# First Strassen product released from the sums of its operand, in a graph network of a GRU stage and three attention layers on one Trainium2 core

## The chip, the core and the metric

The kernel runs on one NeuronCore of a Trainium2 chip. The engines that work here are TensorE (PE in the profile; PEld is its weight loads), VectorE (DVE), ScalarE (ACT), GpSimd (POOL) and SyncE (SP), which issues the DMAs. The metric is the device time of one launch in microseconds, the median of several runs; lower is better.

## The reference, cut to what matters

The input x has 128 graphs of 128 nodes with 256 features, adj has 128 adjacency matrices of 128 x 128. Layer 0 is a gated graph network of three steps with shared GRU weights; layers 1 to 3 are graph attention layers. Each layer adds its input and normalises.

```python
A = (adj != 0).astype(x.dtype); h = x
for i in range(3):                                   # layer 0
    m = jnp.einsum('bnd,de->bne', h, weight[i])
    aggr = jnp.einsum('bst,bsd->btd', A, m)
    gi = aggr @ w_ih.T + b_ih;  gh = h @ w_hh.T + b_hh     # 3 gates of 256: r, z, n
    r = sigmoid(i_r + h_r); z = sigmoid(i_z + h_z)
    n = tanh(i_n + r * h_n); h = (1.0 - z) * n + z * h
x = layernorm(x + h)
for W, a1, a2 in layers_1_to_3:
    Wh = jnp.einsum('bnf,of->bno', x, W)
    e = leaky_relu((Wh @ a1)[:, :, None] + (Wh @ a2)[:, None, :])
    alpha = softmax(where(adj == 0, -inf, e), axis=2)
    x = layernorm(x + alpha @ Wh)
```

## The kernel before

**Tiling and stages.** Four graphs make a group (G), 32 groups (NG) pass through the kernel. Each group goes through six stages: three GRU steps (`gru`, stages 0 to 2) and three attention layers (`gat`, stages 3 to 5). Inside `gru` the features stand on the partitions, in two tiles of 128 features (KC = 2) by 512 columns, which are 4 graphs times 128 nodes. A step first multiplies the hidden state by the adjacency into a `bank` of PSUM (L702 from three bf16 parts with DMA transposes, or L705), copies the result to SBUF, and then computes the gates; weight[i] is multiplied into w_ih once, at the start (L459).

**The Strassen forms.** Each step has two gate products, and each is computed by a Strassen-like scheme (`strassen`, from L621): the 2 x 2 blocks of weights are seven prepared combinations (A11, A12, N22, S1 to S4, in `whs` for the hidden state and `wcs` for the aggregate), and the moving operands are four 128 x 256 pieces of the data plus four differences of them. The differences are made by `sums` (L608, on POOL or DVE) in a tile of four parts, each part built on earlier ones; part 3 is the last. The first form holds gates r and z and adds hidden and aggregate sides, so a product has four matmuls; the second holds the n gate, with two.

Three PSUM buffers of tag `gate` serve a form: bx takes A11, then S2, S3 and N22 on top; bz takes S1, then S4; by takes A12. Between these, the contents of a bank are read out: `kept` copies A11 of bx (`whole`, L716, or `halves`, L720 and L723, on ACT), and `add` (L644, DVE) combines a bank with a kept part. A product that adds into bx or bz can only start when the copy before it has read the bank. There are five gate banks; the three of a form are claimed so that a form can always be finished.

**What sets the order.** No engine chooses at run time. Every operation is put into `Plan` with the engines that may run it and an estimated duration, the buffers that it reads, writes and needs room for, and a priority `prio = stage(g, n)`. `Plan.order` lays all operations out on all engines and writes each engine's instructions in that order. It repeats this for seven passes with due times from the pass before, and keeps the layout that it holds to be shortest. Four inputs matter here:

- `keys` in `product` (L632 to L635): what a block product has to have before it may start. `first` is true of the first product into a bank (A11, S1, A12), and those wait for part 3 of each side's sums too, though A11 itself reads only a piece of the untouched data.
- `own`: buffers of each tag that the planner leaves free for the oldest unfinished half of a group (first dictionary: GRU halves, second: attention halves).
- `LATER`: the offset of each of the six stages in units of a group, added to the group's number as its priority; smaller is earlier. Groups 28 to 31 (LAST = 4) use another rule.
- the estimated TensorE duration of a group of 12 bf16 matmuls (L702), set at the call on L707.

Of the kernel before, what the change touches and what calls it, by code (L numbers as in the profile page):

```python
# [308 lines left out]
def adj_resnorm_kernel(  # L309
# [24 lines left out]

    pools = {"gru": 4, "xs": 2, "am": 5, "k2": 27, "k4": 18, "f": 3, "mv": 4, "st": 6, "v": 36,
             "mb": 4, "gate": 5, "bank": 3}
    own = ({"k2": 8, "k4": 10, "gate": 1, "bank": 0, "v": 5, "st": 0}, {"k2": 3, "k4": 2, "bank": 0, "v": 5, "st": 0})
    floats = {"gru": 0, "k4": 1024, "xs": 1024, "f": 128, "mv": 8, "st": 6, "v": 4, "mb": GN // 2}
    tags = {t: (n, floats.get(t, 512)) for t, n in pools.items()}
    U16, BF16 = mybir.dt.uint16, mybir.dt.bfloat16  # L340
    BOTH = ("DVE", "POOL")
    LATER = (0.25, 1.75, -0.5, 0.75, 0, -0.5)
    plan = Plan({t: n for t, (n, _) in tags.items()}, own)
    slots = {t: [(psum if t in ("gate", "bank") else work).tile([P, w], F32, name=f"{t}{i}")
                 for i in range(n)] for t, (n, w) in tags.items() if w}
# [1 line left out]
    def T(b):  # L347
        if b.at is None:
            width = 1
            for s in b.shape:  # L350
                width *= s
            at = slots[b.tag][b.slot][:, 0:width]
            if len(b.shape) == 2:
                at = at.rearrange("p (a b) -> p a b", b=b.shape[-1])
            elif len(b.shape) == 3:
                at = at.rearrange("p (a b c) -> p a b c", b=b.shape[-2], c=b.shape[-1])
            b.at = at
        return b.at

    def bank():  # L360
        return Buf("bank", GN)
# [16 lines left out]
    A11, A12, N22, S1, S2, S3, S4 = range(7)  # L378
# [23 lines left out]
    def copy(e, dst, src):  # L402
        if e == "ACT":
            nc.scalar.copy(dst, src)  # L404
        else:
            nc.vector.tensor_copy(dst, src)  # L406
# [205 lines left out]
    def moving(m, ms):  # L612

        half = {A11: (0, 0), A12: (1, 0), S4: (1, 1)}
        if m in half:
            c, j = half[m]
            return ms[0][c], lambda: T(ms[0][c])[:, j * H:(j + 1) * H]
        j = {S1: 0, S2: 1, S3: 2, N22: 3}[m]
        return (ms[1], j), lambda: T(ms[1])[:, j, :]

    def strassen(gates, kept, prio):  # L621

        bx, by, bz = Buf("gate", GN), Buf("gate", GN), Buf("gate", GN)
        bx.unit = by.unit = bz.unit = (bx, by, bz)
        o0, o1 = Buf("k4", 2, GN), Buf("k4", 2, GN)
        p1, u2, p5 = Buf("k2", GN), Buf("k2", GN), Buf("k2", GN)

        def product(dst, m, first, *room):  # L630
            todo = [(j, gt, w, ms) for j, (gt, sides) in enumerate(gates) for w, ms in sides]
            keys = {moving(m, ms)[0]: 0 for _, _, _, ms in todo}  # L632
            keys.update({(w, m): 0 for _, _, w, _ in todo})
            if first:
                keys.update({(ms[1], 3): 0 for _, _, _, ms in todo})  # L635

            def fn(e):
                for n, (j, gt, w, ms) in enumerate(todo):
                    nc.tensor.matmul(T(dst)[:, j * H:(j + 1) * H], T(w)[:, m, gt, :], moving(m, ms)[1](),  # L639
                                     start=first and n == 0, stop=n == len(todo) - 1, skip_group_check=True)  # L640
            plan.op({"PE": 431.7 * len(todo)}, fn, reads=list(keys), writes=[dst], prio=prio, room=room)

        def add(b_, part, o, j):
            plan.op({"DVE": 602}, lambda e: nc.vector.tensor_add(  # L644
                T(o)[:, :, j * H:(j + 1) * H], T(b_).rearrange("p (g n) -> p g n", g=2),
                T(part).rearrange("p (g n) -> p g n", g=2)),
                reads=[b_, (part, 0), (part, 1)], writes=[(o, j)], prio=prio)


        product(bx, A11, True, p1)  # L650
        kept(p1, bx, 0)
        product(bz, S1, True, p5)
        kept(p5, bz, 1)
        product(bx, S2, False, u2)
        kept(u2, bx, 0)
        product(bz, S4, False, o0)
        add(bz, u2, o0, 1)
        product(bx, S3, False, o1)
        add(bx, p5, o1, 1)
        product(by, A12, True)  # L660
        add(by, p1, o0, 0)
        product(bx, N22, False)
        return o0, o1, bx

    def gru(g, stage):

        xs, am = Buf("xs", G, D), Buf("am", G, P)
        prio = stage(g, 0)
# [4 lines left out]
                writes=[am], prio=prio)  # L673
        if g == 0:
# [3 lines left out]
                reads=[am], writes=[am, turn], prio=prio, port=BOTH)  # L678
        by_thirds = g < NG - LAST
        if by_thirds:  # L680
            low = Buf("mb", GN // 2)
# [7 lines left out]
        h = None  # L689
        for i in range(STEPS):  # L690
            prio = stage(g, i)
# [3 lines left out]
            for c in range(KC):  # L695
                b_, a_ = bank(), Buf("k2", GN)

                def fn(e, b_=b_, c=c, h=h):
                    for b in range(G):
                        if by_thirds and h is not None:  # L700
                            for j in (2, 1, 0):
                                nc.tensor.matmul(T(b_)[:, b * P:(b + 1) * P], h[1](c, b, j), narrow(b), start=j == 2, stop=j == 0)  # L702
                            continue
                        src = T(xs)[:, b, c * P:(c + 1) * P] if h is None else T(h[c])[:, b, :]
                        nc.tensor.matmul(T(b_)[:, b * P:(b + 1) * P], src, T(am)[:, b, :], start=True, stop=True)  # L705
                if by_thirds and h is not None:
                    plan.op({"PE": 12 * 58}, fn, reads=[low, h[0][c], h[0][2]], writes=[b_], prio=prio, room=[a_])  # L707
                else:
                    plan.op({"PE": 4 * 222.7}, fn, reads=[am, xs if h is None else h[c]], writes=[b_], prio=prio, room=[a_])
                plan.op(EVICT, lambda e, b_=b_, a_=a_: copy(e, T(a_), T(b_)), reads=[b_], writes=[a_], prio=prio)  # L710
                agg.append(a_)
# [17 lines left out]
            for c in range(KC):  # L729

                o, v, d = rz[c], nn[c], Buf("k2", GN)
# [4 lines left out]
                for gt in range(2):  # L736
                    if c == 0:
                        plan.op({"ACT": 614}, lambda e, gt=gt, o=o, tanh=tanh: tanh(gt, 0, GN, lambda: T(o)[:, gt, :]),
                                reads=[(o, 0), (o, 1)], writes=[(o, 2 + gt)], prio=prio)
                    else:  # L740
                        plan.op({"ACT": 357}, lambda e, gt=gt, tanh=tanh, rz=rz: tanh(
                            gt, 0, H, lambda: T(rz[2])[:, gt * H:(gt + 1) * H]),
                            reads=[rz[2]], writes=[(o, 4 + gt)], prio=prio)
                        plan.op({"ACT": 400}, lambda e, gt=gt, o=o, tanh=tanh: tanh(gt, H, GN, lambda: T(o)[:, gt, H:GN]),
                                reads=[(o, 1), (o, 4 + gt)], writes=[(o, 2 + gt)], prio=prio)
                if c == 1:
                    plan.op({"ACT": 357}, lambda e, v=v, nn=nn: nc.scalar.activation(
                        T(v)[:, 0, 0:H], T(nn[2])[:, 0:H], AF.Identity, bias=bhn[:, 1:2]),
                        reads=[nn[2]], writes=[(v, 0)], prio=prio)
                plan.op({"DVE": 602}, lambda e, o=o, v=v: nc.vector.scalar_tensor_tensor(  # L750
                    T(v)[:, 0, :], T(o)[:, 0, :], 1.0, T(v)[:, 0, :], op0=ALU.add, op1=ALU.mult),
                    reads=[(o, 2), (v, 0), (v, 1)], writes=[(v, 2)], prio=prio, port=BOTH)
                if c == 0:
                    plan.op({"DVE": 602}, lambda e, v=v: nc.vector.tensor_add(T(v)[:, 0, :], T(v)[:, 1, :], T(v)[:, 0, :]),
                            reads=[(v, 2)], writes=[(v, 3)], prio=prio, port=BOTH)
                else:
                    plan.op({"DVE": 334}, lambda e, v=v, nn=nn: nc.vector.tensor_add(
                        T(v)[:, 0, 0:H], T(nn[2])[:, H:GN], T(v)[:, 0, 0:H]),
                        reads=[(v, 2), nn[2]], writes=[(v, 3)], prio=prio)
                    plan.op({"DVE": 334}, lambda e, v=v: nc.vector.tensor_add(  # L760
                        T(v)[:, 0, H:GN], T(v)[:, 1, H:GN], T(v)[:, 0, H:GN]),
                        reads=[(v, 2)], writes=[(v, 4)], prio=prio, port=BOTH)
                plan.op({"ACT": 614}, lambda e, v=v, c=c: nc.scalar.activation(  # L763
                    T(v)[:, 0, :], T(v)[:, 0, :], AF.Tanh, bias=bin_[:, c:c + 1]),
                    reads=[(v, 3), (v, 4)], writes=[(v, 5)], prio=prio)
# [3 lines left out]
                    reads=[hT[c], (v, 5)], writes=[d], prio=prio, port=BOTH)  # L769
                plan.op({"DVE": 602}, lambda e, d=d, o=o: nc.vector.scalar_tensor_tensor(  # L770
                    T(d), T(o)[:, 1, :], 1.0, T(d), op0=ALU.add, op1=ALU.mult),
                    reads=[(o, 3), d], writes=[d], prio=prio, port=BOTH)
                plan.op({"DVE": 602}, lambda e, d=d, v=v: nc.vector.scalar_tensor_tensor(  # L773
                    T(d), T(d), 0.5, T(v)[:, 0, :], op0=ALU.mult, op1=ALU.add),
                    reads=[d, (v, 5)], writes=[d], prio=prio, port=BOTH)
                hT2.append(d)
            if i == 0 and by_thirds:
                plan.op(ROUND, lambda e: copy(e, T(low).bitcast(BF16), T(am).rearrange("p b t -> p (b t)")),
                        reads=[am], writes=[low], prio=prio, port=BOTH)
# [9 lines left out]
            for c in range(KC):  # L789
                if last and H3 and 0 < g < NG - LAST:  # L790
# [4 lines left out]
                        writes=[(y, b) for b in range(G)], prio=prio, port=BOTH)  # L795
# [3 lines left out]
                b_ = bank()  # L799
# [5 lines left out]
                if last:  # L805
# [3 lines left out]
                        writes=[(y, b) for b in range(G)], prio=prio)  # L809
# [3 lines left out]
            if not last:  # L813
                h, hT = h2, hT2
# [151 lines left out]
    def stage(g, n):  # L966

        tail = NG - LAST
        return g + LATER[n] if g < tail else tail + n, 2 * g + (n >= STEPS)

    for g in range(NG):
        gat(g, *gru(g, stage), stage)
# [50 lines left out]
```

## Time and profile before

| | |
|---|---|
| median of 3 runs | 2514.24 us (2511.61 to 2514.96) |
| profiled execution | 2513.29 us |
| its span, from the first to the last instruction | 2511.5 us |
| mean granted TensorE clock | 0.998 |
| busy: PE, PEld | 98%, 87% of the span |
| busy: DVE, ACT, POOL | 88%, 76%, 45% |
| DMA | 161.39 MB, mean 64 GB/s |

A group of instructions in the profile is named by line, engine, operation and tiles, and followed by its busy time, the mean duration of one in ns and the idle time of the engine just before it, with what ended that idle time. An fp32 matmul of the program shows as two records in the trace. The tag k stands for all SBUF work buffers, v for the small ones. Recorded matmuls overlap each other, and so do recorded operations of ACT and DVE to a smaller degree.

### The profile page before, as it was taken

Reading aid. Unit: us, or ns where it says so; the run is one execution under the profiler, and the core shown is the slowest. Engines: PE = TensorE matmul, PEld = TensorE weight load, DVE = VectorE, ACT = ScalarE, POOL = GpSimd, SP = SyncE. Lnnn points to the kernel's source line nnn. Section 1 sums busy time; section 2 is a strip of 40 time slices with the busy share of each in tenths; the row PEclk is TensorE's granted clock in tenths of the full one; section 3 lists DMA queues with packets and bytes.
Section 4 is the critical chain, followed back from the end, with each engine's and each line's share of the span. In section 5 each row is a group of like instructions: output and inputs, shape, how many; then the busy total and the mean of one; then the engine's idle time right before and its main releaser. Section 6 shows DMA issues by size and latency. Waiting matters only on the chain. (4 is left out here: it accounts for less than half of the span.)

```text
span 2511.5 us, 42493 instructions
## 1 busy us (share of the span) xinstructions
PE 2470.1 (98%) x13492; PEld 2183.0 (87%) x13492; DVE 2198.2 (88%) x6149; ACT 1897.7 (76%) x4799; POOL 1122.9 (45%) x1329
## 2 busy tenths in 40 slices
PE   8999999999999999999999999999999999999988
PEld 7888888888888888888888888888888888888877
DVE  6778888988898998998988989989989999977797
ACT  5567778788787787877788787788887777675578
POOL 3443554554545554444534445544445553524211
PEclk9999999999999999999999999999999999999999
DMA  4222333333323333333333333332333332110101
GB/s 139 63 58 52 68 68 67 73 72 68 72 59 73 76 75 62 76 72 67 76 69 64 76 61 74 68 76 64 64 82 61 80 69 59 39 35 17 39 1 35
DMA packets 456610, 161.39 MB, mean 64 GB/s; under 512 B 389184, under 2 KB 454720, under 8 KB 456384
## 3 DMA queue, kind: packets, MB, share of 16 engines
q1 hardware_dynamic: 455952, 158.65, 29.0%
q8 instruction: 106, 1.74, 0.3%
q14 instruction: 120, 0.98, 0.1%
q10 hardware_dynamic: 432, 0.01, 0.0%
HBM read 45.89 MB, written 16.78 MB: 25 GB/s over the span
## 5 line engine op out<-in xcount | busy, mean ns | idle before, releaser
L639 PE MATMUL gate<-k,whs 128*128 128x256 f32 x4032 | 1206.8, 381 | 13.0 <-ACT k L716 5.6
L639 PE MATMUL gate<-k,wcs 128*128 128x256 f32 x4032 | 1199.3, 379 | 0.6 <-ACT wcs L404 0.6
L639 PEld LDWEIGHTS gate<-k,wcs 128*128 128x128 f32 x4032 | 766.0, 190 | 105.0 <-ACT wcs L404 1.0
L639 PEld LDWEIGHTS gate<-k,whs 128*128 128x128 f32 x4032 | 742.7, 190 | 121.4 <-ACT k L716 14.6
L608 POOL TENSOR_TENSOR k<-k,k 128x256 f32<-128x256 f32 x493 | 425.0, 875 | 209.3 <-DVE k L773 51.7
L644 DVE TENSOR_TENSOR k<-gate,k 128x512 f32<-128x512 f32 x576 | 391.1, 684 | 111.5 <-PE gate L639 79.5
L948 PE MATMUL bank<-gwT,k 128*128 128x256 f32 x1536 | 349.8, 380 | 1.4 <-DVE k L406 0.8
L831 DVE SCALAR_TENSOR_TENSOR nobody<-k,wa 128x256 bf16<-128x256 f32 x768 | 339.2, 473 | 3.8 <-ACT k L574 3.4
L555 POOL TENSOR_TENSOR v<-v,neghalf 128x4 f32<-128x4 f32 x128 | 149.6, 1171 | 426.4 <-DVE v L593 204.7
L948 PEld LDWEIGHTS bank<-gwT,k 128*128 128x128 f32 x1536 | 289.5, 190 | 42.8 <-DVE k L406 2.4
L734 ACT ACTIVATE k<-k,brz 128x256 f32<-128x256 f32 (+1 forms) x384 | 226.8, 624 | 72.8 <-DVE k L644 72.6
L608 POOL TENSOR_TENSOR k<-k 128x256 f32<-128x256 f32 x170 | 151.8, 895 | 255.0 <-DVE k L773 104.7
L716 ACT COPY k<-gate 128x512 f32<-128x512 f32 x288 | 166.2, 579 | 93.7 <-PE gate L639 92.1
L768 POOL TENSOR_TENSOR k<-k,k 128x512 f32<-128x512 f32 x89 | 118.3, 1330 | 259.2 <-ACT k L763 234.3
L850 POOL PARTITION_BROADCAST k<-k x336 | 160.8, 573 | 156.1 <-ACT k L404 77.2
L582 ACT ACTIVATE nobody<-k 128x256 bf16<-128x256 f32 x384 | 156.7, 410 | 84.7 <-DVE k L954 84.2
L404 ACT COPY k<-bank 128x512 f32<-128x512 f32 (+1 forms) x280 | 147.3, 530 | 94.6 <-PE bank L843 35.1
L954 DVE SCALAR_TENSOR_TENSOR k<-bank,v,k 128x256 f32<-128x256 f32 x384 | 167.5, 476 | 41.2 <-PE bank L948 40.3
L937 PEld LDWEIGHTS bank<-k,k 128*128 128x128 f32 x1536 | 187.8, 193 | 12.9 <-ACT k L503 4.0
L503 ACT COPY k<-k 128x1024 uint16<-128x1024 uint16 x152 | 175.8, 1163 | 26.8 <-DMA k<-k 24.8
L937 PE MATMUL bank<-k,k 128*128 128x128 f32 x1536 | 190.9, 277 | 5.2 <-ACT k L503 2.5
L763 ACT ACTIVATE k<-k,bi 128x512 f32<-128x512 f32 x192 | 138.0, 723 | 43.7 <-DVE k L760 24.3
(109 smaller groups left out, 3457.0 us busy)
## 6 DMA issues: line engine op xcount, KB each, us to landing
xs<-in_x_dram SPq DMA_DIRECT2D x32, 512.0 KB, 3.9
k<-in_x_dram SPq DMA_DIRECT2D x32, 512.0 KB, 4.1
out_dram<-k SPq DMA_DIRECT2D x32, 512.0 KB, 3.0
am<-in_adj_dram SPq DMA_DIRECT2D x32, 256.0 KB, 2.9
k<-k SPq DMA_TRANSPOSE x366, 3.1
k<-in_gnn_wT_dram SPq DMA_DIRECT2D x3, 256.0 KB, 4.8
k<-in_w_ihT_dram SPq DMA_DIRECT2D x2, 384.0 KB, 6.2
k<-in_w_hhT_dram SPq DMA_DIRECT2D x2, 384.0 KB, 7.1
```

Source lines behind the costliest of these rows:

```text
L503: nc.scalar.copy(flat().bitcast(U16).rearrange("p (q h) -> p q h", h=2), T(rows).bitcast(U16).rearrange("p (h q) -> p q h", h=2))
L582: plan.op({"ACT": 400}, lambda e, b=b: nc.scalar.activation(next(nobody[0]), T(y)[:, b, :], AF.Square, accum_out=T(ss)[:, b:b + 1]), reads ...
L608: nc.vector if e == "DVE" else nc.gpsimd).tensor_tensor(T(t)[:, j, :], a(), b(), ALU.subtract),
L639: nc.tensor.matmul(T(dst)[:, j * H:(j + 1) * H], T(w)[:, m, gt, :], moving(m, ms)[1](), start=first and n == 0, stop=n == len(todo) - 1, s ...
L644: plan.op({"DVE": 602}, lambda e: nc.vector.tensor_add(T(o)[:, :, j * H:(j + 1) * H], T(b_).rearrange("p (g n) -> p g n", g=2), T(part).re ...
L716: plan.op({"ACT": 475}, lambda e: nc.scalar.copy(T(dst), T(src)), reads=[src], writes=[(dst, 0), (dst, 1)], prio=prio)
L734: nc.scalar.activation(T(o)[:, gt, n0:n1], src(), AF.Tanh, bias=brz[:, gt * KC + c:gt * KC + c + 1], scale=0.5)
L831: plan.op({"DVE": 345}, lambda e, b=b, h=h, l=l, side=side, xc=xc: nc.vector.scalar_tensor_tensor(next(nobody[1]), T(xc)[:, b, :], 1.0, T( ...
L850: plan.op({"POOL": 292}, lambda e, row=row, b=b, e_=e_: nc.gpsimd.partition_broadcast(T(e_)[:, b, :], T(row)[b * P // G:b * P // G + 1, 0: ...
L937: nc.tensor.matmul(T(b_)[:, b * P:(b + 1) * P], T(xc)[:, b, c * P:(c + 1) * P], T(pT)[:, b, :], start=True, stop=True)
L948: nc.tensor.matmul(T(b_)[:, (b - b0) * D:(b - b0 + 1) * D], T(aT[k])[:, b * P:(b + 1) * P], T(gwT)[:, l, k, :], start=(k == 0), stop=(k == ...
L954: nc.vector.scalar_tensor_tensor(T(y)[:, b, :], T(b_)[:, (b - b0) * D:(b - b0 + 1) * D], T(rden)[:, b:b + 1], T(xc)[:, b, :], op0=ALU.mult ...
```

## The change

```diff
-    own = ({"k2": 8, "k4": 10, "gate": 1, "bank": 0, "v": 5, "st": 0}, {"k2": 3, "k4": 2, "bank": 0, "v": 5, "st": 0})
+    own = ({"k2": 7, "k4": 10, "gate": 0, "bank": 0, "v": 5, "st": 0}, {"k2": 3, "k4": 2, "bank": 0, "v": 4, "st": 0})
...
-    LATER = (0.25, 1.75, -0.5, 0.75, 0, -0.5)
+    LATER = (0.25, 1.75, -1.0, 0.25, 0, -0.5)
...
-            if first:
+            if first and m != A11:
                 keys.update({(ms[1], 3): 0 for _, _, _, ms in todo})
...
                 if by_thirds and h is not None:
-                    plan.op({"PE": 12 * 58}, fn, reads=[low, h[0][c], h[0][2]], writes=[b_], prio=prio, room=[a_])
+                    plan.op({"PE": 12 * 55.6}, fn, reads=[low, h[0][c], h[0][2]], writes=[b_], prio=prio, room=[a_])
```

The product A11 of each form no longer needs part 3 of the sums of its moving operands; S1 and A12 still do. The GRU halves leave free one k2 buffer less and no gate bank, the attention halves one v buffer less. The third GRU step and the first attention layer get earlier priorities. The estimated duration of the 12 bf16 matmuls falls from 696 to 667 ns. All computation is the same; what differs in the built program is the order in which instructions stand on each engine, the engine of a few dozen of them, the buffers that they use, and the waits that follow from these.

## The prediction

> **What bounds the kernel now.** I read the page's busy time and slices first, then PE's list of waits, the busy table of three stretches, the groups, and a timeline of the longest stop. From the page:
>
> ```profile
> span 2511.5 us, 42493 instructions
> PE 2470.1 (98%) x13492; PEld 2183.0 (87%) x13492; DVE 2198.2 (88%) x6149; ACT 1897.7 (76%) x4799; POOL 1122.9 (45%) x1329
> PE   8999999999999999999999999999999999999988
> ...
> L639 PE MATMUL gate<-k,whs 128*128 128x256 f32 x4032 | 1206.8, 381 | 13.0 <-ACT k L716 5.6
> L608 POOL TENSOR_TENSOR k<-k,k 128x256 f32<-128x256 f32 x493 | 425.0, 875 | 209.3 <-DVE k L773 51.7
> L644 DVE TENSOR_TENSOR k<-gate,k 128x512 f32<-128x512 f32 x576 | 391.1, 684 | 111.5 <-PE gate L639 79.5
> ```
>
> TensorE is full in 37 of 40 slices; no other engine is. The program issues the same matmuls after the change, so only TensorE's stops can move the time, and the question is how large they are. The busy sum hides part of them: a record lasts 379 to 381 ns, while the next one starts 216 ns later (the chain of waits has "PE gate L639 x16" as 3.45 us). I therefore count by pitch: 9,600 records of L639 and L948 at 0.2159 us, 2,176 of L937 and L705 at 0.1116, 1,344 of L702 at 0.0558, 300 transposes at 0.109 and 20.7 us of weight products make 2,443.4 us. The first matmul starts at 5.1 and the last starts 8.8 before the end, so 2,511.5 - 2,443.4 - 13.9 = 54 us are stops. Put where the starts fall apart, they are 5.8 us in the first 60 us, 33.5 in the middle (to about 2,395) and 14.4 in the rest. The busy table agrees in shape (idle 7.4, 18.6, 16.0; each stop there is shortened by the overhang of the record before it):
>
> ```profile
> 0.00:60.00 60.00, 52.65 (x231) 41.60 (x232) 39.43 (x83) 33.71 (x61) 17.40 (x26) 1.00 0.50 145
> 60.00:2395.00 2335.00, 2316.43 (x12683) 2053.20 (x12681) 2060.82 (x5595) 1775.46 (x4413) 1087.36 (x1287) 1.00 0.30 64
> 2395.00:2512.00 117.00, 100.99 (x580) 88.17 (x580) 97.93 (x473) 88.54 (x327) 18.15 (x18) 0.95 0.06 19
> ```
>
> Its columns are length, then busy time and count of PE, PEld, DVE, ACT, POOL, then clock. What TensorE stops for, from its list of waits:
>
> ```profile
> PE gate L639 <- ACT k L716: 5.6, 8, 2.2
> PE gate L639 <- DVE k L644: 4.4, 7, 1.3
> PE bank L937 <- ACT k L503: 2.5, 4, 0.9
> PE gate L639 <- ACT k L723: 2.3, 3, 1.1
> ```
>
> The three L639 rows are the Strassen chain against itself: a product adds into a gate bank that ACT (L716, L720, L723) or DVE (L644) must have read first. The longest stop, in the timeline:
>
> ```profile
> 984.40 1.04 ACT L404 COPY k<-xs 128x1024 uint16<-128x1024 uint16 x1 [3.50 <-DMA xs<-in_x_dram]
> 985.35 1.06 ACT L716 COPY k<-gate 128x512 f32<-128x512 f32 x2
> ...
> 985.99 0.70 PE L639 MATMUL gate<-k,whs 128*128 128x256 f32 x2 [2.19 <-ACT k L716]
> ```
>
> ACT waited 3.5 us for a load of x, and the eviction that the next product needs stood behind it.
>
> **What the Trainium skill says.** "TensorE: Matmul & The Clock Gate", section "Wait — 56ns, not 53.3ns?", gives about 55.6 ns between warm 128-column bf16 matmuls; here 24 of L702 take 1.34 us, 55.8 each. Its section "Architectural detail" says that ACT and DVE take their instructions strictly in order; the 3.50 us above show it. "Perfetto Trace Analysis", section "Tensor Engine Instruction", says that a matmul's recorded end is an estimate, hence the count by pitch. The first page's "What's actually happening" has the clock halve after idle of about 3.4 us; the trace shows 0.93 of the clock in 2400 to 2450 and 1.00 in the middle.
>
> **The change, part by part.** Every line issues the same number of instructions over all engines (20,208 in both). Between engines a few dozen move: by the rows' means DVE gets 25 sums of L608 (+14 us), loses 11 subtractions of L528 (15 bf16 at 0.79 less 4 at 0.84: -8.5) and gains about 2 in copies and scalings, so +8 on 2,198; POOL -12, ACT -1. Over 2,511 us that is 0.3%, and DVE has 12% free in the whole: nothing, except in the last 80 us.
>
> *The changed price of L702's groups* (12 x 58 to 12 x 55.6 ns) is the planner's alone. The measured 12 x 55.8 is 670 ns; the plan assumed 696 and will assume 667. No run time by itself.
>
> *The key not taken for A11.* Before, A11 stood in the order directly before S1, the second product, in 52 of the 96 forms of gates r and z and in 73 of the 96 of gate n. After it, that is so in 7 and 33; the mean TensorE work between the two grows from 1.5 to 3.9 us and from 1.1 to 9.6. The bank of A11 has to be read out before S2 adds into it. In form n, S1 covers 2 x 0.432 = 0.86 us, and the two evictions (back to back 0.36 + 0.25) with 0.2 us of hand-off on either side need 1.0. The move gives exactly this eviction time. It costs no issue; it holds a bank longer (A11's start to the seventh product's end: 20.7 to 22.2 us, and 13.7 to 21.2).
>
> *The reserves and offsets* (steps taken earlier; gate reserve 0) only reorder, as does the first edit, so I price the three together, from the order in which both programs' instructions stand. For each matmul group that waits, I took the helper that it waits for and went back, through data or through that helper's queue, to the TensorE group from which the work started. The work on that way, at the back-to-back pitch of its rows (L644 0.60 us, L406 0.60, L716 0.48, L831 0.34, L608 on POOL 0.75) plus 0.2 us of hand-off, less TensorE's work in between, is its shortfall; negative, it is spare time. The hand-off is the record's overhang, 379 - 216 ns, plus some 50 ns from a recorded end to the next start. No stop is put into TensorE's side, so this gives no time by itself. What a wait of each class costs comes from the trace of before. In the middle:
>
> | | waits before | lost in the trace, us | mean, us | waits after | at that mean, us |
> |---|---|---|---|---|---|
> | short by any amount | 25 | 14.5 | 0.58 (0.50 up to 0.5 short) | 5 | 2.5 |
> | spare 0 to 0.5 | 107 | 3.7 | 0.035 | 63 | 2.2 |
> | spare 0.5 to 1 | 343 | 9.4 | 0.027 | 336 | 9.2 |
> | spare 1 to 3 | 608 | 4.6 | 0.007 | 718 | 5.4 |
> | spare over 3 | 680 | 0.3 | 0 | 606 | 0.3 |
>
> So 32.5 us become 19.5, a gain of 13. The largest shortfall goes from 1.3 to 0.1 us; 54 of the 25 + 107 were S2, S4 and N22 of form n (31 of 68 after). S2 of form n has 43 waits after, for 86. I don't take all 13: the means were read off the plan that had these stops, and the classes with spare time (14 us of loss) stop for things that no order shows, such as the load of x. ACT waited for such loads 13.9 us in 8 places, and only one cost TensorE 2 us; the SP queue's loads and transposes now stand elsewhere in its order, which I bound by -2 and +5. I take two thirds, 9 us.
>
> *The last 80 us* are DVE's: the chain of waits there is nearly all DVE rows. By the same count DVE runs 12.2 us behind TensorE at worst before (14.4 measured, with the slow clock). After, DVE has 85.0 us of work left where TensorE has 80 (83.2 before), and runs 14.1 behind: +1.5 to +2. The first 60 us differ only in where 8 weight products stand: 4.4 us by either order, nothing.
>
> Sum: -9 + 1.5 = -7.5 us, span 2,504. The profiled execution took 2,513.3 for its 2,511.5; the median of the runs is 2,514.2, 0.9 more. So 2,514.2 - 7.5, rounded: **2,506.5 us**. 0.2%, 5 us, is about what a measurement can tell from no change: below 2,509.2 is faster, above 2,519.3 slower.
>
> **The rivals.**
>
> *The stops come back elsewhere* (0.23): 1,054 waits have 0.5 to 3 us to spare; if their mean cost grows by 0.008 us, because other loads and POOL results come late, 8 us of the gain go. For it: no order tells these. Against: the classes are about as full as before. 2,514, between 2,509 and 2,519.
>
> *S1 waits for POOL instead* (0.12, slower): A11 no longer vouches for S1's sums, so a late sum stops TensorE with the bank already taken, and 192 forms have an S1. Place: S1 behind L608, whose row lasts 0.88 us where the plan counts 0.69, so four in a row come 0.75 us later than planned. For it: 54 S1 waits of form r, z hang on POOL. Against: by my count, at POOL's measured pitch, only one S1 of these and none of form n has less than 0.5 us to spare, and six in all have less than 1. It decides once it eats the gain of 7.5 and 5 more, 0.065 us per form; at 0.1 us, 19 us, it ends at 2,526. DVE's longer tail could add to it but alone gives 2.
>
> *The order does nothing that counts* would need the same stops; it is excluded, since nearly every row of each engine's order differs, and belongs to the first rival.
>
> The likeliest has 0.65, with its own range of 2,498 to 2,511: 2,501 is the full 13 less the tail, 2,498 adds what earlier loads could give. The whole range, with the first rival in it and the second left out, is 2,497 to 2,519. Faster 0.66, within 0.2% 0.21, slower 0.13.
>
> **What would show it.** Right: L639's waits for ACT L716, L723 and DVE L644, 12.3 us before, fall to under 7; TensorE's idle in 60 to 2395 falls from 18.6 to 11 to 14; its busy table's last 117 us stay within 2 us. A new row "L639 <- POOL L608" above 3 us, or waits for DMA on PE or ahead of ACT L716, would make the first or second rival right; a last stretch with over 18 us idle would show that the tail was mis-sized.

## The result and the profile after

The changed kernel takes 2,498.26 us (median of 4 runs, 2,497.32 to 2,499.11) against 2,514.44 (2,511.61 to 2,514.96) before: a ratio of 0.9938, interval 0.9921 to 0.9955, 16.2 us faster. The forecast was 2,506.5 with a range of 2,497 to 2,519: the right sign, and inside the range by 1.3 us at its fast end; the forecast change, 7.7 us, is only half of the measured one.

The first lines of the page after, to be set against those shown of before:

```profile
span 2497.3 us, 42426 instructions
PE 2466.9 (99%) x13492; PEld 2182.1 (87%) x13492; DVE 2200.0 (88%) x6167; ACT 1896.6 (76%) x4798; POOL 1099.4 (44%) x1312
PE   9999999999999999999999999999999999999998
...
L644 DVE TENSOR_TENSOR k<-gate,k 128x512 f32<-128x512 f32 x576 | 391.9, 684 | 112.4 <-PE gate L639 85.1
L608 POOL TENSOR_TENSOR k<-k,k 128x256 f32<-128x256 f32 x474 | 399.2, 857 | 174.8 <-ACT k L404 55.9
```

TensorE still runs 13,492 records, and its matmuls are no faster (L639's records last 381 and 379 ns, as before). The span is 14.2 us shorter. By pitch, as in the prediction, TensorE's stops went from 54 us to 39.7. The busy table of the three stretches (length, then busy time and count of PE, PEld, DVE, ACT, POOL, clock, DMA share, GB/s):

```profile
0.00:60.00 60.00, 53.80 (x239) 43.42 (x240) 39.69 (x81) 34.09 (x59) 19.47 (x26) 1.00 0.51 147
60.00:2380.00 2320.00, 2311.78 (x12673) 2050.06 (x12671) 2062.40 (x5610) 1772.98 (x4416) 1058.81 (x1267) 1.00 0.31 65
2380.00:2498.00 118.00, 101.31 (x584) 88.64 (x582) 97.95 (x477) 89.54 (x325) 21.15 (x20) 0.94 0.06 19
```

In the middle TensorE's recorded idle is 8.2 us where it was 18.6; in the last stretch it is 16.7 for 16.0. By pitch: first stretch 4.2 us (before 6.1), middle 20.7 (33.5), last 14.8 (14.4). (The prediction had 5.8 for the first; 6.1 counts the matmuls at the very start too, from which no chain goes back.) TensorE's list of waits after:

```profile
...
PE bank L803 <- DVE k L773: 2.7, 1, 2.7
PE gate L639 <- DVE k L644: 2.6, 6, 1.0
PE gate L639 <- ACT k L716: 2.2, 4, 1.1
...
PE gate L639 <- ACT k L723: 1.0, 3, 0.6
```

The three rows of L639 fell from 12.3 us to 5.8. That A11 now runs while its own sums are being made can be seen in the timeline of one step (TensorE's rows, then POOL's and DVE's of L608):

```profile
590.99 0.60 PE L639 MATMUL gate<-k,whs 128*128 128x256 f32 x2
591.43 0.59 PE L639 MATMUL gate<-k,wcs 128*128 128x256 f32 x2
...
592.03 1.91 POOL L608 TENSOR_TENSOR k<-k,k 128x256 f32<-128x256 f32 x2 [0.87 <-DVE k L406]
...
592.40 0.95 DVE L608 TENSOR_TENSOR k<-k,k 128x256 f32<-128x256 f32 x1
```

The product that starts at 590.99 is an A11 of gates r and z (found by its place in TensorE's order); the last of its aggregate's sums ends at 593.9, and S1 starts at 596.18; a product of another form, A11 of form n and this form's S2 run in between. Followed through the trace, the last sum of the aggregate ends after A11 has started in 86 of the 96 forms of r and z, for 18 before. That there are 18 at all shows what kind of hold it was: the plan placed A11 behind the sums' expected end, but A11 doesn't read them, and on the chip it didn't wait for them. Where this text says that A11 waits or is held, it is held in the plan.

### The profile page after: what moved, and what is told of

Same layout as the page of the kernel before. It is cut to its first block, busy times and chain, and to the rows that moved or that the text cites. A ratio compares the mean times of both kernels' runs of the same rounds, so it can differ in the third digit from the quotient of the medians.

```text
span 2497.3 us, 42426 instructions
## 1 busy us (share of the span) xinstructions
PE 2466.9 (99%) x13492; PEld 2182.1 (87%) x13492; DVE 2200.0 (88%) x6167; ACT 1896.6 (76%) x4798; POOL 1099.4 (44%) x1312
## 5 line engine op out<-in xcount | busy, mean ns | idle before, releaser
L639 PE MATMUL gate<-k,whs 128*128 128x256 f32 x4032 | 1206.5, 381 | 6.0 <-DVE k L644 2.6
L639 PE MATMUL gate<-k,wcs 128*128 128x256 f32 x4032 | 1199.3, 379 | 0.6 <-ACT wcs L404 0.6
L639 PEld LDWEIGHTS gate<-k,wcs 128*128 128x128 f32 x4032 | 766.0, 190 | 105.1 <-ACT wcs L404 1.0
L639 PEld LDWEIGHTS gate<-k,whs 128*128 128x128 f32 x4032 | 740.9, 190 | 111.9 <-DVE k L644 6.9
L608 POOL TENSOR_TENSOR k<-k,k 128x256 f32<-128x256 f32 x474 | 399.2, 857 | 174.8 <-ACT k L404 55.9
L608 POOL TENSOR_TENSOR k<-k 128x256 f32<-128x256 f32 x164 | 146.2, 893 | 372.1 <-DVE k L773 107.7
L734 ACT ACTIVATE k<-k,brz 128x512 f32<-128x512 f32 (+1 forms) x384 | 226.3, 623 | 73.9 <-DVE k L644 73.5
L716 ACT COPY k<-gate 128x512 f32<-128x512 f32 x288 | 167.4, 582 | 116.9 <-PE gate L639 113.7
L404 ACT COPY k<-bank 128x512 f32<-128x512 f32 (+1 forms) x283 | 151.0, 536 | 89.6 <-PE bank L843 30.3
L850 POOL PARTITION_BROADCAST k<-k x336 | 154.1, 558 | 124.4 <-ACT k L404 66.0
L503 ACT COPY k<-k 128x1024 uint16<-128x1024 uint16 x153 | 177.4, 1162 | 33.9 <-DMA k<-k 33.5
L937 PEld LDWEIGHTS bank<-k,k 128*128 128x128 f32 x1536 | 187.8, 193 | 8.6 <-ACT k L503 1.7
L937 PE MATMUL bank<-k,k 128*128 128x128 f32 x1536 | 190.3, 277 | 2.6 <-ACT k L404 1.2
```

The source lines that it names most:

```text
L503: nc.scalar.copy(flat().bitcast(U16).rearrange("p (q h) -> p q h", h=2), T(rows).bitcast(U16).rearrange("p (h q) -> p q h", h=2))
L608: nc.vector if e == "DVE" else nc.gpsimd).tensor_tensor(T(t)[:, j, :], a(), b(), ALU.subtract),
L716: plan.op({"ACT": 475}, lambda e: nc.scalar.copy(T(dst), T(src)), reads=[src], writes=[(dst, 0), (dst, 1)], prio=prio)
L734: nc.scalar.activation(T(o)[:, gt, n0:n1], src(), AF.Tanh, bias=brz[:, gt * KC + c:gt * KC + c + 1], scale=0.5)
L850: plan.op({"POOL": 292}, lambda e, row=row, b=b, e_=e_: nc.gpsimd.partition_broadcast(T(e_)[:, b, :], T(row)[b * P // G:b * P // G + 1, 0: ...
L937: nc.tensor.matmul(T(b_)[:, b * P:(b + 1) * P], T(xc)[:, b, c * P:(c + 1) * P], T(pT)[:, b, :], start=True, stop=True)
```

## The experiments

The question was which edit brings the gain, through which form, and whether it is one lucky layout of the planner. T1 is that the released A11 brings it in whatever form, as TensorE work that is ready while the sums are made; T2 the prediction's own mechanism, that in form n the eviction of A11 gets time before S2; T3 that the reserves and offsets bring it. "Short waits" are those of the prediction's table, counted in the middle from the order alone; stops are counted by pitch, from the traces.

### One part at a time

**e1**, the key alone:

```diff
 (kernel before)
-            if first:
+            if first and m != A11:
```

> The kernel before with one edit: A11 no longer waits for part 3 of the sums; reserves, offsets and the estimate of L702 as before. T1 (the released A11 gives nearly all of the gain, in whatever form): by the count of short waits 4 are left in the middle (25 before, 5 after the whole change), so TensorE's stops there fall from 33.5 to about 20 us, the last stretch is up to 2 us worse, and the median is 2,500 to 2,506 us. T3 (reserves and offsets carry the gain): 2,511 to 2,518, with the middle's stops at 30 or more.

Measured: 2,497.58 us, ratio 0.9938 (0.9924 to 0.9953), 4 short waits, 19.4 us of stops in the middle. This is the whole gain; T3 falls. The time is below the 2,500 to 2,506 of T1.

**e2**, all but the key:

```diff
 (changed kernel)
-            if first and m != A11:
+            if first:
```

> The changed kernel with the key taken back: A11 waits for part 3 again, with the new reserves, offsets and estimate. T1: 18 short waits, 28 us of stops in the middle, the last stretch 2 to 5 us worse: 2,509 to 2,517 us. T3: 2,498 to 2,503, as the whole change.

Measured: 2,525.62 us, ratio 1.0050 (1.0035 to 1.0065): slower than before by 12 us, where T1 expected at most 2,517. The stops in the middle are 41.7 us and not 28, and the last stretch has 21.0. Its list of waits:

```profile
PE gate L639 <- ACT k L716: 17.4, 22, 2.1
...
PE gate L639 <- DVE k L644: 5.2, 7, 1.3
```

L716 reads the bank of A11, S1 or S2 in the form of r and z. S2 of this form, which needs A11's bank read, alone stops for 16.4 us (5.9 before, 1.4 after the change). In this layout A11 stands directly before S1 in 58 of 96 of those forms, so that S1's 1.73 us may be all that covers the eviction. But it does so in 54 before as well: why S2 stops three times as long here isn't shown.

**e3**, the key in the form of r and z only, and **e4**, in the form of n only:

```diff
 (e3: kernel before)
-            if first:
+            if first and (m != A11 or gates[0][0] == 2):
 (e4: kernel before; the reserve is needed for an order to be found at all)
-    own = ({"k2": 8, "k4": 10, "gate": 1, "bank": 0, "v": 5, "st": 0}, {"k2": 3, "k4": 2, "bank": 0, "v": 5, "st": 0})
+    own = ({"k2": 7, "k4": 10, "gate": 1, "bank": 0, "v": 5, "st": 0}, {"k2": 3, "k4": 2, "bank": 0, "v": 5, "st": 0})
-            if first:
+            if first and (m != A11 or gates[0][0] == 0):
```

> The kernel before with A11 released only in the form of gates r and z; in the form of gate n A11 stays directly before S1 in 81 of 96 forms. T1 (more TensorE work ready while the sums are made): 5 short waits, 21 us of stops in the middle, 2,501 to 2,508 us. T2 (the prediction's way: the eviction of A11 in form n gets cover before S2): the n form is as before, so most of the gain is missing, 2,510 to 2,516, and the rows L639 <- ACT L716, L723 stay near 8 us.

> The kernel before with A11 released only in the form of gate n, and the k2 reserve of the GRU halves at 7 as after the change, without which no order can be laid out. A11 stands 21 us of TensorE work ahead of S1, directly before it in only 8 of 96 forms. T2: the gain is here, 2,499 to 2,506 us. T1: 24 short waits are left, 33 us of stops in the middle, 2,511 to 2,518 us.

Measured: e3 2,496.82 us, ratio 0.9937 (0.9922 to 0.9952), 14.6 us of stops in the middle, both below what T1 expected; e4 2,511.98, ratio 0.9995 (0.9986 to 1.0004), 30.3 us. The form of r and z carries the gain and the form of n none of it, so T2 falls, though e4 moved A11 of n further ahead than the change does. The "in whatever form" of T1 falls too; what held in both was the count of short waits.

The code suggests why. Both forms of a step use the same sums: `h_in` and `a_in` are made once and passed to both. In the order of before, A11 of n stands behind A11 of r and z in all 96 steps, so its place came after the sums that the other had waited for. In e4, where only r and z still wait, A11 of n goes ahead of it in 80 of 96 steps, and 21 us of TensorE work stand between it and its S1, while it keeps a gate bank. That this bank is what e4 pays with is not shown.

**e5**, A11 held by the first of the four sums instead of the last:

```diff
 (kernel before)
-                keys.update({(ms[1], 3): 0 for _, _, _, ms in todo})
+                keys.update({(ms[1], 0 if m == A11 else 3): 0 for _, _, _, ms in todo})
```

> The kernel before, but A11 waits only for part 0 of the sums (the first of four) instead of part 3. T1 in its graded form (the earlier A11 may start, the fewer short waits): between the two, 17 short waits in the middle and 27 us of stops by the count, 2,504 to 2,511 us. If only the full release counts (any hold on the sums undoes it): 2,511 to 2,518. If one part is as good as all: 2,496 to 2,501.

Measured: 2,515.39 us, ratio 1.0012 (1.0005 to 1.0018), 35.4 us of stops in the middle. The count had promised 27 and 2,504 to 2,511; that is a miss. Waiting for one sum of each side already brings TensorE's stops back to before's level in this layout. Yet A11 of r and z starts before the last sum of the aggregate in 76 of 96 forms here, exactly as in e3, and S2 of r and z stops for only 0.9 us; the loss is in the form of n, whose products stop for 18.3 us (7.2 before, 6.2 after the change). So an A11 that runs while its sums are made isn't enough for the gain. As it is one layout, and held layouts differ by far more than this (next), it doesn't settle how small a hold can be before it hurts.

### One layout or all of them

A plan that is searched for changes everywhere when an input moves by a hair. Four kernels have a change in the planner's numbers alone, which changes no computation:

```diff
 (e6: kernel before)  -  {"PE": 12 * 58}       +  {"PE": 12 * 55.6}
 (e7: kernel before)  -  MARGIN = 300          +  MARGIN = 305
 (e12: kernel before) -  MARGIN = 300          +  MARGIN = 295
 (e8: changed kernel) -  MARGIN = 300          +  MARGIN = 305
```

> The kernel before with only the estimate of L702's groups at 667 ns instead of 696; A11 still waits. Nothing in it changes a duration on the chip. By the count of short waits: 50 in the middle (25 before), 47 us of stops, 2,522 to 2,534 us. If layouts without the release all cost about the same on the chip: 2,511 to 2,518.

> The kernel before with the planner's margin at 305 ns instead of 300, a change without meaning that draws another layout. A11 waits. By the count: 44 short waits, the largest 6.5 us, 44 us of stops, 2,518 to 2,531 us. If the count says nothing within one setting: 2,511 to 2,518.

> The kernel before with the planner's margin at 295 ns, the held layout with the fewest short waits of those laid out (20) and DVE 12.1 us behind in the last stretch. A11 waits. By the count 30 us of stops in the middle: 2,507 to 2,515 us. If held layouts can be as good as released ones by luck: 2,496 to 2,503.

> The changed kernel with the planner's margin at 305 ns, another layout. A11 is released. If the release is the cause and not one lucky layout: 3 short waits, 19 us of stops in the middle, 2,495 to 2,502 us, as the change. If the change was a lucky draw: 2,505 to 2,520.

Measured: e6 2,543.87 us (ratio 1.0127, 1.0112 to 1.0142); e7 2,548.60 (1.0143, 1.0128 to 1.0158); e12 2,514.63 (1.0007, 0.9998 to 1.0015); e8 2,494.72 (0.9930, 0.9913 to 0.9946). e6 and e7 went the way that the count said, and further than its ranges. e12's time is in its range, but its stops are 36.9 us for the 30 counted, and with 20 short waits it isn't the held layout with the fewest (e2 has 18). e8 is at the fast end of what the release let expect and far from the 2,505 to 2,520 of a lucky draw. In e7 the largest shortfall, 6.5 us by the count, is the longest stop of TensorE:

```profile
PE bank L937 <- ACT k L897: 12.6, 4, 10.1
PE gate L639 <- ACT k L716: 9.0, 15, 1.5
```

Two more layouts of the released kernel were chosen for their counts:

```diff
 (e9: changed kernel)  -  RATHER = 600                               +  RATHER = 650
 (e10: changed kernel) -  LATER = (0.25, 1.75, -1.0, 0.25, 0, -0.5)  +  LATER = (0.25, 1.75, -0.75, 0.5, 0, -0.5)
```

> The changed kernel with the planner's preference for DVE over POOL at 650 ns instead of 600 (RATHER), chosen for its count: 2 short waits in the middle and the least delay of DVE in the last stretch (13.6 us where the change has 14.1). If the count ranks layouts finely: 2,490 to 2,496 us, the fastest so far. If it only tells held layouts from released ones: 2,494 to 2,501.

> The changed kernel with the stage offsets at -0.75 and 0.5, half way between before and after. 2 short waits, DVE 14.6 us behind in the last stretch. The offsets matter little once A11 is released: 2,492 to 2,500 us. If the offsets of the change are needed: 2,505 or more.

Measured: e9 2,498.18 us (0.9941, 0.9926 to 0.9955), so the count does not rank the released layouts among themselves; e10 2,495.07 (0.9928, 0.9913 to 0.9943), so the change's offsets are not needed. e8 and e10 have the lowest medians of all, 3 us under the change. That is less than a measurement can tell from no change, and the intervals of their ratios overlap that of the change.

### Further release

**e11** takes the hold from S1 and A12 as well:

```diff
 (changed kernel)
-            if first and m != A11:
+            if False:
```

> The changed kernel with S1 and A12 released from part 3 of the sums too (S1 still needs the part that it reads). If more released work gives still fewer stops: 1 short wait, 20 us in the middle, but DVE 19 us behind in the last stretch, 2,496 to 2,505 us. If it is A11 alone that counts, the same or slower; if the hold on S1 and A12 guards the chain from stopping with its banks taken: over 2,506.

Measured: 2,511.73 us, ratio 0.9994 (0.9985 to 1.0002), above the 2,496 to 2,505 expected if more release is better. By the time alone one would say that the hold on S1 and A12 guards the chain, for which over 2,506 had been expected. The busy table says otherwise; whole stretches of e11, then ten microseconds of its end:

```profile
1200.00:1600.00 400.00, 398.88 (x2206) 354.25 (x2205) 362.35 (x1004) 313.92 (x785) 187.44 (x225) 1.00 0.33 70
1600.00:2000.00 400.00, 398.72 (x2199) 354.28 (x2198) 359.27 (x1016) 310.22 (x788) 212.49 (x247) 1.00 0.34 70
2000.00:2390.00 390.00, 390.00 (x2103) 348.61 (x2102) 336.02 (x886) 271.97 (x688) 148.32 (x182) 1.00 0.19 42
2390.00:2510.00 120.00, 93.45 (x505) 80.46 (x503) 86.95 (x440) 81.18 (x306) 16.45 (x15) 0.86 0.06 19
```

```profile
2400.00:2410.00 10.00, 7.99 (x37) 6.66 (x36) 7.41 (x27) 7.55 (x31) 1.26 (x1) 0.54 0.00 0
```

The middle is the best of all kernels, 13.5 us of stops; the last stretch has 33.6 instead of 14.8. TensorE's idle there is 26.6 us and the granted clock 0.86, as low as 0.54 in the ten microseconds shown. How these four groups are laid out at the end ate the gain of the middle. About 9 of the 33.6 us are matmuls at a lowered clock, for about 3 of the 14.8 after the change (an estimate from their starts, 427 ns apart instead of 216). Whether the release does this or this one layout is not shown. The prediction's count gave DVE 19.2 us of delay here for the 14.1 of the change, the right sign and about a quarter of the size. In the middle of e11 A11 stands directly before S1 in 45 forms of r and z and 70 of n, nearly as often as before (54 and 74), so the distance between the two isn't what a good middle needs.

### All layouts side by side

| kernel | A11 of r, z | short waits | stops in the middle, us | last stretch, us | median, us |
|---|---|---|---|---|---|
| before | held | 25 | 33.5 | 14.4 | 2,514.4 |
| e12 margin 295 | held | 20 | 36.9 | 12.8 | 2,514.6 |
| e2 settings only | held | 18 | 41.7 | 21.0 | 2,525.6 |
| e4 n only | held | 24 | 30.3 | 18.4 | 2,512.0 |
| e5 part 0 | held by one sum | 17 | 35.4 | 16.3 | 2,515.4 |
| e6 estimate only | held | 50 | 63.2 | 14.6 | 2,543.9 |
| e7 margin 305 | held | 44 | 65.3 | 18.4 | 2,548.6 |
| after | released | 5 | 20.7 | 14.8 | 2,498.3 |
| e1 key only | released | 4 | 19.4 | 15.6 | 2,497.6 |
| e3 r, z only | released | 5 | 14.6 | 18.4 | 2,496.8 |
| e8 margin 305 | released | 3 | 16.6 | 13.4 | 2,494.7 |
| e9 RATHER 650 | released | 2 | 21.9 | 14.4 | 2,498.2 |
| e10 offsets | released | 2 | 15.9 | 14.7 | 2,495.1 |
| e11 no holds | released | 1 | 13.5 | 33.6 | 2,511.7 |

The kernel before, run again beside these, gave 2,512.8 to 2,513.5 us; each ratio above is to those runs. Seven layouts with A11 of r and z held have 30 to 65 us of stops in the middle, seven with it released have 14 to 22. So the release of this A11 is the cause of the fewer stops, not the draw; e11 shows that the time can still be lost at the end.

Two things qualify the table. First, the expected stops of the middle were within 7 us for the four released layouts that had such a number (20, 21, 19 and 20 for e1, e3, e8 and e11), but in the held ones they were too low by 7 to 21 us, e4 apart, and among held layouts of 17 to 25 short waits the count doesn't rank. Second, stops by pitch contain slowed matmuls: the granted clock fell to a half in the middle of six of the seven held layouts (not of the kernel before), for 3.4 us in e2 and e4, 6.8 in e5 and e12, 10.2 in e6 and 17.1 in e7. By the starts of the matmuls in these stretches this made 1.6 to 4.8 us of their stops, an estimate. In the middle of the released ones the clock never fell.

## Why the prediction was right or wrong

- *What bounds the kernel.* Right: all matmuls kept their pitch, and the 14.2 us of the span are stops, 12.8 of them in the middle.
- *The table of short and spare waits.* Right here, and better than I trusted it. It gave 19.5 us for the waits after; they lost 19.7: 1.1 in the 5 short ones (2.5 forecast), 3.5 with up to 0.5 us to spare (2.2), 9.3 up to 1 (9.2), 4.3 up to 3 (5.4), 1.5 beyond (0.3). That the sums agree to 0.2 us is in part luck, since the same count missed by up to 21 us in other layouts.
- *"I take two thirds, 9 us".* This is the term that was mis-sized. The reason given, that classes with spare time stop for things that no order shows, called for no discount: the classes with more than 0.5 us to spare lost 14.3 us before and 15.1 after. The middle gave 12.8. (The bound of the likeliest range has a slip as well: the full 13 less the tail of 1.5 is 2,502.7, not 2,501.)
- *The last 80 us.* +1.5 expected, +0.4 measured by pitch, 0.7 more recorded idle: too pessimistic by about 1 us.
- *The first 60 us.* Expected nothing; they gave 1.9. No run asks why.
- The rest of the difference, 2 us, is the runs' median against the profiled executions: 16.2 between medians, 14.2 between spans, well within the scatter of the runs.
- *The mechanism named for the key*, eviction time for A11 in form n: wrong, shown by e3 and e4. The step that failed took the move of n's A11 (1.1 to 9.6 us ahead of S1) for the gain because it was the larger one, while the order of before already showed A11 of n behind A11 of r and z in every step. (Counted again, the orders have A11 directly before S1 in 54 and 74 forms before and in 7 and 41 after, for the prediction's 52, 73, 7 and 33; the argument is the same.) So the sign of the forecast came from the count over the whole order, which doesn't rest on that mechanism; as far as the mechanism goes, the right sign was luck.
- *The same eviction time in the form of r and z* is part of the gain: S2 there stops for 5.9 us before and 1.4 after, and L937, an attention matmul, for 5.4 and 1.7. Over all layouts, S2 of r and z stops for 5.9 to 16.4 us in before, e2, e6, e7 and e12 and for at most 2.9 in the seven released ones, but also for only 1.4 in e4 and 0.9 in e5, which lose elsewhere. A likely reading is that a ready A11 fills TensorE's order where it would have had to take something that was not ready; no run shows this by itself, and e5 speaks against its simplest form. The mechanism stays open beyond S2.
- *The estimate of L702, "no run time by itself".* True of the matmuls, whose records are no faster, wrong as a statement on the edit: alone it costs 31 us (e6), since it draws another layout. Together with the release and the other settings it costs nothing that shows (e1 against the change).
- *The three edits priced together.* Right to do: they don't add. Without the key the settings lose 12 us, with it they make no difference that can be measured.
- *The rivals.* Stops that come back elsewhere: they did not, the classes with spare time lost what they had lost. S1 waiting for POOL: there is no such row in the list of waits; S1's stops are 0.2 us.
- *What would show it.* L639's waits under 7: 5.8. The middle's idle was to be 11 to 14; it was 8.2, with the gain under-sized above. Last stretch within 2 us: it was. The sign for the rivals is small: L702 waits 0.9 us for a DMA, where no such row stood before.

## What to carry to other kernels

When the order is the whole change, and the bound engine is full, count for each of its waits how much of its own work stands between the wait and the work from which the wait's chain started; the trace of the kernel before gives what each class of shortfall costs, and here that count told the good orders from the bad ones before a run, though not two good ones from each other, nor the held ones of 17 to 25 short waits. A dependency that is stricter than the data needs may pay in one of its places only: here its removal gave the whole gain in the form of r and z and none in that of n, so try each place by itself. And a searched plan moves as a whole, so one run of one setting says little; compare families of layouts.

## What the runs showed of the hardware

- Held layouts that differ from the kernel before in one planner constant by 2 to 4% ran 29 and 34 us slower (2,543.9 and 2,548.6 us for 2,514.4) with the same computation, and one ran level (2,514.6). The layout alone, with 50 and 44 short waits for 25, makes that much.
- Stops cost clock as well as time, and a stop need not be long for it. In e4 a single wait of 2.2 us (2.4 by pitch) in dense work was followed by 3.4 us at half the clock, in which 16 records of L937 took 3.22 us; such a group takes 1.95 in the kernel before (at 1,699.93 us). In the kernel before, the stop of 2.2 us at 983 us left the clock at 1.00:

```profile
1248.00:1251.00 3.00, 0.77 (x6) 0.37 (x5) 2.11 (x8) 2.36 (x8) 0.00 (x0) 1.00 0.01 1
1251.00:1254.00 3.00, 3.00 (x18) 3.00 (x17) 2.31 (x6) 3.00 (x8) 0.81 (x2) 0.55 0.00 0
...
1250.85 3.22 PE L937 MATMUL bank<-k,k 128*128 128x128 f32 x16
...
983.00:986.00 3.00, 0.81 (x5) 0.38 (x3) 1.60 (x2) 1.60 (x3) 2.92 (x4) 1.00 0.08 24
986.00:989.00 3.00, 3.00 (x14) 2.62 (x15) 2.65 (x7) 1.90 (x4) 2.30 (x3) 1.00 0.91 174
```

- In e6 a stop of 1.8 us (at 635 us) was followed by a fall of the clock (0.50 from 639 to 641), while one of 3.2 us (at 179 us) was not (1.00 from 183 to 190). So the length of a stop alone doesn't tell whether the clock falls; what does is not shown. The stretches at half clock that ended inside the work lasted 3.4, 6.8, 10.2 or 17.1 us, multiples of about 3.4.
- In e11 no wait of TensorE in the last 100 us is longer than 3.0 us, yet the granted clock was 0.54, 1.00, 0.98, 0.85, 1.00, 1.00 and 0.66 in successive stretches of 10 us from 2,400.
